# Six buffers instead of five for the residual rows of a graph-attention layer that runs ahead of a slice mixer

## The chip, the cores and the metric

The kernel runs on one core of a Trainium2 chip. The metric is the device time of one launch in microseconds, the median over several runs. TensorE does matrix products and transposes, VectorE and ScalarE work elementwise, GpSimd (POOL in the profile) does small powers and issues the gathering, casting and accumulating transfers, and SyncE (SP) issues the other transfers.

## What is computed

Two layers over `x` (32 batches of 512 rows of 256 numbers, float32), with an adjacency matrix of 512 x 512 integers for each batch:

```python
# layer 0
x = x + relu(layernorm(x) @ W_upd + mean_over_neighbours(layernorm(x) @ W_msg) + bias)
x = x + ffn(layernorm(x))            # tropical max-plus branch gated with a GELU branch
# layer 1
x = x + graph_attention(layernorm(x), adj)   # 4 heads of 64, softmax over neighbours,
                                             # relu + residual, layernorm per head
x = x + slice_mixer(layernorm(x))            # softmax of rows to 64 slices for each of 8 heads,
                                             # a scan over the 64 slice tokens, rows back from slices
```

Within one batch, layer 1 needs all 512 rows of layer 0's result. The batches are independent.

## The kernel before, in words

`layer0_sorted` computes layer 0 with the rows sorted, and writes them to DRAM tensors `x2s`; `ranks` holds where each row went. `layer1_plain` (L865) computes layer 1 and writes `out`. A general version of both layers stands behind a condition at the end and does not run on these inputs. The change is in `layer1_plain` alone.

Layer 1 handles the 32 batches by pairs (`GB = 2`). The mixer of pair g, `mixer(g)`, calls `slices(b)` for its two batches, then `tokens` and `scan` for both together, then `unslice(b)` for each. Beside it, `attentions()` runs ahead: for each batch `prepare(b)`, `attention(b)` and `norm(b)`, with the attention of batch b mixed step by step with the preparation of batch b + 1 by `woven`. The mixer's steps earn credit (`PACE`, L896), and each unit of credit advances `attentions()` by a step (L1581 to L1589). So the program's order is fixed when it is built; a tile scheduler then sets the semaphores, and the order of each engine's instructions does not change at run time.

What the steps do, with the lines that matter here:

- `prepare(b)`, L1136 on: takes a tile `x` of [128, 4, 256] float32 (512 KB, 4 KB in each partition) that holds the residual rows of the batch, and gathers the rows with four indirect transfers on POOL (L1142). `turn(b)` (L1091, SP) transposes the adjacency mask, and `shorten(b + 2)` (L1085, POOL) copies the adjacency of a later batch to a shorter type, as tile `short`. Then a normalisation: statistics `stc`, `mvc` on VectorE (L1114, L1115), the deviation `rsc` on POOL (L30, L31), `shiftc` on VectorE (L1119), the normalised rows `hv` on ScalarE (L1121). `add_rows` (L953, POOL) adds the vector BETA to the residual rows with an accumulating transfer. Transposes x3T (L1130, L1131) and the projection `hp` (L1171) follow; for each of four row tiles ScalarE makes `hv`, `mine`, `other` and `ht` (L1174 to L1179) and VectorE scales `hv` (L1175). `own` is sent to DRAM and read back for each of four heads as a broadcast (L1190, SP).
- `attention(b)`: weights `att` on VectorE (L1201), products `avp` and `adp` on TensorE (L1237, L1242), back-transposes `dp` and `bp` (L1220), `av` on VectorE (L1265), and another `add_rows` into `av`.
- `norm(b)`, L1274 on: the norm of each head, on VectorE (L1282 to L1286, L1290, L1291, L1293, L1295), with a square on ScalarE (L1288) and a power on POOL (L1292, tile `mu`). Last, L1296 adds the rows `av` to the residual tile `x`.
- `slices(b)`: normalisation as above with tiles `std`, `mvd`, `rsd`, `shiftd`; transposes x4T; `add_rows` with OUTB; for each of four row tiles t the logits `lgp` on TensorE (L1327), the exponential on ScalarE (L1328) and the softmax on VectorE (L1329, L1332, L1333, L1334, tile `sw`); then `yTp` (L1339), which contracts the rows of a batch against `sw`, for two halves c of the features, and the transposes `swp` (L1344).
- `tokens` and `scan`: projections and a scan over the slices, among them the transposes `oTp` (L1527) near the end.
- `unslice(b)`: products `outp` (L1559), added to the residual tile (L1561), and one store of 512 KB to `out` (L1562, SP). Then b is put in the set `stored` (L1563).

The residual tile of a batch lives from its gather to its store. `AHEAD_X` is the number of these tiles, and it also holds a preparation back in the program's order:

```python
while b >= AHEAD_X and b - AHEAD_X not in stored:
    yield True
xt = xs[b] = sb.tile([P, NT, D], F32, tag="x", name=f"x{b}", bufs=AHEAD_X)
```

A step that yields True gives the turn away: `woven` goes on with the attention alone, and when that has ended too, the credit is set to zero. With five tiles, batch 2g + 5 is prepared after the first store of pair g, and batch 2g + 6 after the second.

Of the kernel before, what the change touches and what calls it, by code (L numbers as in the profile page):

```python
# [864 lines left out]
def layer1_plain(tc, ident, eps, x2s, ranks, adj, w, out, over, ps):  # L865
# [6 lines left out]
    GB = 2  # L872
# [19 lines left out]
    AHEAD = 3  # L892
    ATT = 2 * (AHEAD + 2) + AP + 1
    HW = P // AH
    AHEAD_X = 2 * GB + 1
    PACE = 1.04 * GB * (TURNS + STEPS) / WANTED  # L896

    SMALL = 30.0 * 30.0 / D
# [2 lines left out]
    with ExitStack() as ctx:  # L901
# [234 lines left out]
        def prepare(b):  # L1136
# [4 lines that stand above are left out]
            for t in range(NT):  # L1141
# [1007 lines left out]
def tile_kernel(ctx, tc, ins, out):  # L2149
# [21 lines left out]
    with tc.tile_pool(name="few", bufs=1) as few:  # L2171
        over = few.tile([P, n0 + n1], F32, tag="over", name="over")
        NSEG = 4
        x2s = [dram.tile([len(x2) // NSEG * N, D], F32, tag=f"x2s_{i}", name=f"x2s_{i}") for i in range(NSEG)]
        ranks = few.tile([P, len(x2) * NT], I32, tag="ranks", name="ranks")
        rest = []

        def following(ps):
            rest.append(layer1_plain(tc, ident, eps2, x2s, ranks, ins["adj"], w1, out, over[:, n0:], ps))
            return iter(lambda: next(rest[0]), True)  # L2180

        layer0_sorted(tc, ident, eps2, ins["x"], ins["adj"], w0, x2s, ranks, over[:, :n0], following)
        for _ in rest[0]:
            pass


        ones = few.tile([P, 1], F32, tag="ones", name="ones")
        nc.gpsimd.memset(ones, 1.0)
        worst = few.tile([P, 1], F32, tag="worst", name="worst")
        nc.vector.tensor_reduce(worst, over, AX.X, ALU.add)  # L2190
        with tc.tile_pool(name="pf", bufs=1, space=PSUM) as ps:
            pf = ps.tile([P, N], F32, tag="flag", name="flag")
            nc.tensor.matmul(pf[:1, :1], worst, ones, start=True, stop=True)
            nc.vector.tensor_copy(again, pf[:1, :1])
# [36 lines left out]
```

## Time and profile before

| what | value |
| --- | --- |
| three runs | 4503.5, 4513.17, 4514.52 us; median 4513.17 |
| the profiled execution | 4515.02 us, its span 4513.3 us, mean granted clock 0.94 |
| TensorE busy | 3933.4 us, 87% of the span |
| VectorE, ScalarE, POOL busy | 3204.0, 2198.0, 1570.2 us |
| layer 1, 2372.0 to 4513.3 us | TensorE busy 1906.2 us in all |
| of it 2600 to 4272 us (steady) | TensorE 1520.4, VectorE 1080.1, ScalarE 725.3, POOL 356.3 of 1672 us; DMA share 0.33 |
| transfers over the span | 524.04 MB, mean 116 GB/s |

How to read it: the span runs from the first to the last instruction; the time of the execution has a little around it. "Busy" counts an engine's instructions without what they wait for. A group's line gives line, engine, operation, output<-input tiles, shapes and count, then busy us, mean ns of one, and the idle time just before them with the instruction that ended it. In a timeline, a line gives start, duration, engine, line and operation, and in brackets the idle time before it with its releaser. In the chain of waits, each piece gives start, duration and what ran; "issue" is time in which the engine waited for nothing that the profile shows. DMA pieces are transfers. The share of the DMA engines is the mean over the core's sixteen. The granted clock is TensorE's, 1.00 being full speed.

In the steady stretch one pair of batches takes about 129 us, and every such period has the same stages: the first slice, the second slice, the scan, and the two stores with the next gathers.

### The profile page before, as it was taken

What the parts mean: (1) busy time and instruction counts of PE and PEld (TensorE: products, weight loads), DVE (VectorE), ACT (ScalarE), POOL (GpSimd) and SP (SyncE); (2) the same over time, 40 slices, a digit from 0 to 9 for tenths busy, and PEclk for the clock granted to TensorE, in tenths of its full rate; (3) what the DMA queues carried; (4) which work ended last, traced back from release to release, by engine and by line L of the source; (5) the groups of instructions that cost most, each with busy time, mean ns of one, the idle gap of its engine ahead of it and who ended that gap; (6) DMA issues with size and microseconds to landing.
All of it is one profiled execution on the core that took longest, in us unless ns stands there. A gap on an engine that the chain in (4) does not pass through costs nothing.

```text
span 4513.3 us, 56135 instructions
## 1 busy us (share of the span) xinstructions
PE 3933.4 (87%) x19799; PEld 2468.0 (55%) x19799; DVE 3204.0 (71%) x6909; ACT 2198.0 (49%) x4305; POOL 1570.2 (35%) x2069
## 2 busy tenths in 40 slices
PE   5567898899988999889997999898998898989987
PEld 4454565656656656555553555555555455555555
DVE  6678888897788877867765766656666666666663
ACT  3345565556565665545663444344444443444433
POOL 2356544664446554444313122222211222222110
PEclk8778999999999999989998999999999999999998
DMA  5546543664446643564315233333322333333210
GB/s 129 160 142 224 184 140 110 206 202 154 135 129 206 194 141 109 169 216 160 129 59 117 52 76 79 80 80 68 83 68 62 73 80 80 80 70 76 62 38 20
DMA packets 301248, 524.04 MB, mean 116 GB/s; under 512 B 104823, under 2 KB 180227, under 8 KB 300956
## 3 DMA queue, kind: packets, MB, share of 16 engines
q0 software_dynamic: 117120, 383.06, 30.6%
q1 hardware_dynamic: 183836, 137.30, 10.4%
q8 instruction: 158, 2.59, 0.2%
q14 instruction: 134, 1.10, 0.1%
HBM read 463.11 MB, written 73.95 MB: 119 GB/s over the span
## 4 chain that ended last, share of the span: by engine, by line
PE 32%; DVE 31%; DMA 15%; issue 9%; POOL 8%; ACT 4%; SPq 1%; DVEq 0%; POOLq 0%; ACTq 0%
DVE acc L637 4%; PE clsp L623 4%; PE po L652 4%; DMA av<-added 3%; PE yTp L1339 3%; PE gatep L623 3%; PE outp L1559 3%; POOL mu L1292 2%; DMA rows<-table,xs 2%; DMA out<-x 2%; DMA rows<-table,tops 2%; DVE best L598 2%; PE oTp L1527 2%; DVE att L1201 2%; PE avp L1237 2%
## 5 line engine op out<-in xcount | busy, mean ns | idle before, releaser
L623 PE MATMUL clsp<-xnT,wc 128*128 128x512 f32 x1024 | 524.8, 631 | 46.7 <-ACT cls L625 34.4
L623 PE MATMUL gatep<-xnT,wg 128*128 128x512 f32 x1024 | 496.8, 605 | 9.3 <-ACT gate L625 9.3
L652 PE MATMUL po<-wd,acc 128*128 128x256 f32 x2048 | 457.3, 382 | 8.4 <-DVE acc L641 5.9
L652 PEld LDWEIGHTS po<-wd,acc 128*128 128x128 f32 x2048 | 389.2, 192 | 75.2 <-issue 9.6
L1201 DVE SCALAR_TENSOR_TENSOR att<-own,other,mask 128x512 f32<-128x512 f32 x512 | 358.3, 737 | 12.8 <-DMA own<-ownd 12.8
L598 DVE SCALAR_TENSOR_TENSOR best<-rows,xs,best 128x1024 f32<-128x1024 f32 x212 | 272.6, 1288 | 126.8 <-ACT best L592 79.5
L637 DVE SCALAR_TENSOR_TENSOR acc<-past,fld,acc 128x512 f32<-128x512 f32 x448 | 344.6, 772 | 23.8 <-ACT past L636 16.0
L1237 PE MATMUL avp<-att,hv 128*32 128x512 f32 x2048 | 333.0, 601 | 7.2 <-DVE att L1201 7.2
L1339 PE MATMUL yTp<-sw,x 128*128 128x512 f32 x512 | 262.1, 666 | 88.0 <-DVE sw L1334 88.0
L623 PEld LDWEIGHTS gatep<-xnT,wg 128*128 128x128 f32 x1024 | 196.8, 196 | 253.3 <-issue 203.5
L632 ACT ACTIVATE acc<-tz,fld 128x512 f32<-128x512 f32 x256 | 198.7, 776 | 279.1 <-PE tz L630 247.4
L636 ACT ACTIVATE past<-tz,fld 128x512 f32<-128x512 f32 x448 | 291.5, 693 | 79.3 <-DVE acc L637 77.7
L595 POOL DMA_INDIRECT rows<-table,xs x212 | 251.5, 1186 | 170.3 <-DVE best L598 117.3
L623 PEld LDWEIGHTS clsp<-xnT,wc 128*128 128x128 f32 x1024 | 183.9, 200 | 185.9 <-issue 114.1
L434 PE MATMUL pm<-h,adj 128*128 128x258 f32 (+1 forms) x1024 | 182.9, 326 | 103.9 <-DVE keep L427 42.6
L1327 PE MATMUL lgp<-wsl,x4T 128*128 128x512 f32 x512 | 241.3, 617 | 22.4 <-ACT x4T L1131 22.4
L625 ACT ACTIVATE gate<-gatep,fld 128x512 f32<-128x512 f32 x256 | 175.4, 685 | 146.4 <-PE gatep L623 124.0
L553 POOL DMA_INDIRECT xs<-rows_of,order x128 | 156.7, 1225 | 215.3 <-DVE acc L637 93.3
L1339 PEld LDWEIGHTS yTp<-sw,x 128*128 128x128 f32 x512 | 104.9, 214 | 227.5 <-DVE sw L1334 126.2
L1559 PE MATMUL outp<-v,swT 128*128 128x256 f32 x1024 | 226.2, 379 | 0.0
L434 PEld LDWEIGHTS pm<-h,adj 128*128 128x128 f32 x1024 | 152.8, 215 | 129.2 <-issue 73.4
L625 ACT ACTIVATE cls<-clsp,fld 128x512 f32<-128x512 f32 x256 | 176.0, 687 | 95.3 <-PE clsp L623 58.8
(593 smaller groups left out, 8550.7 us busy)
## 6 DMA issues: line engine op xcount, KB each, us to landing
adj<-in_adj POOLq DMA_DIRECT2D x128, 256.0 KB
x<-added POOLq DMA_DIRECT2D x64, 512.0 KB
own<-ownd SPq DMA_DIRECT2D x128, 256.0 KB
rows_of<-keep SPq DMA_DIRECT2D x32, 550.0 KB
x<-in_x SPq DMA_DIRECT2D x32, 512.0 KB
x2s<-xs SPq DMA_DIRECT2D x32, 512.0 KB
short<-in_adj POOLq DMA_DIRECT2D x32, 512.0 KB
av<-added POOLq DMA_DIRECT2D x32, 512.0 KB
```

Of the source, the lines that this page charges most:

```text
L434: nc.tensor.matmul(pm[:, : c1 - c0], a[:, i, t * P : (t + 1) * P], h[:, i, c0:c1], start=i + c0 == 0, stop=i + 1 == NT and c0 > 0)
L595: nc.gpsimd.indirect_dma_start(out=row, out_offset=None, in_=table, in_offset=bass.IndirectOffsetOnAxis(ap=idxs[:, k : k + 1].bitcast(U32) ...
L598: nc.vector.scalar_tensor_tensor(m, row, vals[:, k : k + 1], m, ALU.add, ALU.max)
L623: nc.tensor.matmul(pf, wf[:, c, f * P : (f + 1) * P], xnT[:, c, :], start=c == 0, stop=c == DC - 1)
L625: nc.scalar.activation(o, pf, fn, bias=fld[:, f, bf : bf + 1], scale=1.0 if fn == AF.Gelu else 0.5)
L636: nc.scalar.activation(r, z, AF.Relu, bias=fld[:, f, AT + b : AT + b + 1])
L637: nc.vector.scalar_tensor_tensor(y, r, fld[:, f, CH + b : CH + b + 1], y, ALU.mult, ALU.add)
L652: nc.tensor.matmul(po[:, i, :], acc[f][:, t * P : (t + 1) * P], wd[:, f, :], start=f == 0, stop=f == FC - 1)
L1201: nc.vector.scalar_tensor_tensor(e, own[h], other[:, j, h : h + 1], mask[:, j, :], ALU.max, ALU.mult)
L1237: nc.tensor.matmul(pv[p][k * HW : (k + 1) * HW, :], hv[:, j, h, e : e + HW], weighed[b, h, j], **ends)
L1339: nc.tensor.matmul(py, xn[:, t, c * P : (c + 1) * P], sw[:, t, :], start=t == 0, stop=t == NT - 1)
L1559: nc.tensor.matmul(po[:, :D], swT[:, k, t * P : (t + 1) * P], v[:, k, :], start=k == 0, stop=k == KC - 1)
```

## The change

One constant grows by one. The tile pool holds six residual tiles, 24 KB of each partition where it held 20, and `prepare(b)` waits for the store of batch b − 6 where it waited for that of b − 5. For batch 2g + 6 that is the first store of pair g. Batch 2g + 7 waits for the second store of pair g; it waited for the first store of pair g + 1 before. Batch 5 waits for no store. What `prepare` yields, and what the steps compute, stays the same; the places of the other steps on the engines follow from the order in which the generators are advanced.

```diff
@@ -892,7 +892,7 @@
     AHEAD = 3
     ATT = 2 * (AHEAD + 2) + AP + 1
     HW = P // AH
-    AHEAD_X = 2 * GB + 1
+    AHEAD_X = 2 * GB + 2
     PACE = 1.04 * GB * (TURNS + STEPS) / WANTED
 
     SMALL = 30.0 * 30.0 / D
```

## The prediction on record

> **What bounds the kernel now.** I read the page first (span, slices, groups), then the waits of TensorE in layer 1, then one pair end by the chain of waits and by the timelines of the engines. The page gives a span of 4513.3 us and this group:
>
> ```profile
> L1339 PE MATMUL yTp<-sw,x 128*128 128x512 f32 x512 | 262.1, 666 | 88.0 <-DVE sw L1334 88.0
> ```
>
> It is the largest idle time of TensorE that is put down to one line of layer 1. The edit touches only `layer1_plain`, which runs from the first gather (L1142, at 2372 us) to the end: some 2141 us. Between 2600 and 4272 us TensorE is busy for 1520 of 1672 us, so it is the bound there, and what counts is what it waits for. Its waits in that stretch (total us, times, longest) begin with:
>
> ```profile
> PE yTp L1339 <- DVE sw L1334: 82.8, 18, 7.5
> PE lgp L1327 <- ACT x4T L1131: 19.5, 13, 3.4
> PE minep L1183 <- ACT mine L1177: 16.8, 13, 1.3
> ```
>
> Nearly all of the 82.8 us lies in one place that comes back every 129 us or so: the end of a pair, where `unslice` has stored two batches and the next pair's first slice starts. The chain of waits through the pair end near 3000 us shows what is late (start, duration, what):
>
> ```profile
> 2990.35 6.86 DMA out<-x
> ...
> 3001.85 0.95 POOL x L1142
> 3002.80 0.61 POOL short L1085
> 3003.40 2.97 POOL mu L1292
> ...
> 3007.54 0.42 DVE stc L1114
> 3007.96 1.12 DVE x L1296
> 3009.09 1.20 DVE sw L1329 x2
> ...
> 3011.71 0.61 DVE sw L1334
> 3012.32 0.04 issue
> 3012.37 9.30 PE yTp L1339 x16
> ```
>
> The reader is to see one queue behind another. POOL waits for the second store of the pair (`out<-x`), because its next gather reuses that buffer. Behind the four gathers stand the adjacency copy `short` and only then the power `mu` of an attention's norm; VectorE waits for `mu`, and the softmax weights `sw` that TensorE needs are queued on VectorE behind it. The timelines give the two idle times, VectorE's and then TensorE's:
>
> ```profile
> 3006.40 1.22 DVE L1295 TENSOR_TENSOR av<-av,mu 128x1024 f32<-128x1024 f32 x1 [8.79 <-POOL mu L1292]
> ```
>
> ```profile
> 3012.37 9.30 PE L1339 MATMUL yTp<-sw,x 128*128 128x512 f32 x16 [6.42 <-DVE sw L1334]
> ```
>
> At thirteen pair ends this idle time is 3.1, 6.0, 6.3, 6.4, 5.9, 6.1, 7.2, 6.6, 6.5, 7.5, 6.5, 6.7 and 5.3 us; at a fourteenth, near 4290, it is 1.7.
>
> [...] `mu` has its input from 2996.2 us on and starts at 3003.40, directly behind the gathers and `short`. [...] granted clock 0.50 or 1.00, a fall 3.1 to 4.9 us after TensorE stops at twelve pair ends, full speed again 3.6 to 6.0 us after it restarts.
>
> **The change, part by part.** I compared the instruction orders of the two kernels. No instruction is added or dropped; some are moved.
>
> *At a pair end.* Before, the batches gathered are an odd one (after the first store) and the next even one (after the second). With six buffers the odd one was gathered a pair earlier, so the two are the even one (first store) and the next odd one (second store). The wait for the second store stays: POOL's gathers still stand ahead of `mu`. Three things leave the path from the second store to `yTp`:
> - `short` goes behind `mu`: −0.60 us (0.61 in the chain).
> - One `stc` statistic, L1114, no longer stands between L1295 and L1329: −0.34.
> - L1296 goes behind all four groups of `sw`: −1.12. It adds an attention's rows to a batch that the next pair needs, so it has time.
>
> Together −2.06 us. Against it: TensorE's order of `yTp` becomes all four row tiles of one half, then of the other. The third tile of `sw` is ready 3.75 us after the first (L1334's second pair of instructions starts at 15.46 against 11.63, from the timeline of VectorE, with 0.64 for one); the four instructions of the first two tiles take about 3.5 at half clock (16 instructions in 7.21 at full clock are 0.45 each, so about 0.9 at half): 0.25 us of waiting. Net −1.8 us for each of 12 pair ends. From `yTp` the chain runs on TensorE to 3033.8 almost without a break, so I count it in full. At the first pair end the idle time is split in two and the clock does not fall; I take −1.2. At the last, near 4290, no odd batch is left to gather; `stc` and its L1115s go from before L1291 (some 1.7 us of VectorE, half of it beside other waits): −1.2 (0 to −1.7).
>
> *What is paid for it.* The odd batch's normalisation (ScalarE, L1121 x4, 2.07 us) moves into the scan, where ScalarE is idle for 1.60 us before L1174 at 3088.30, and its BETA add (POOL, 0.5 MB) moves behind the other add of the scan. I cost both at nothing: the idle time hides the first but for some 0.1 to 0.5 us, and VectorE's idle time of 7.90 us before 3096.86 hides the second. If that cover is gone, see the fourth case. SP's queue keeps its order.
>
> *At the start.* Batch 5 is now gathered at once. Four gathers and a `short` enter POOL at about 2414.5 us, ahead of an add and the L30/L31 of batch 3: 4 x 1.25 (their spacing there) + 0.6 = 5.6 us, and 0.5 MB of rows and 1 MB of adjacency read beside `own<-ownd`, for which the first attention waits:
>
> ```profile
> 2414.53 1.04 POOL L953 DMA_DIRECT2D x<-added  x1
> 2415.36 0.43 POOL L30 TENSOR_TENSOR rsc<-mvc,eps 128x4 f32<-128x4 f32 x1
> ```
>
> VectorE also meets the `stc` of batch 5 ahead of the first `att` at 2423.41, and so waits for those rows. The trace of before does not show this; bounds: +1.5 us (1.5 MB more at the page's mean would take far longer, but most of it is not waited for) to +6 (the whole POOL block and 0.35 of L30/L31). I take +3.4, nearer the middle.
>
> *Sum.* −(1.2 + 12 x 1.8 + 1.2) + 3.4 = −20.6 us, against the profiled execution's 4515.02: 4494.4. That execution lies 1.85 us above the median of the three runs (4513.17), so the forecast for the median is 4492.6.
>
> **The rivals.**
> - *A: given back.* Only `short` is gained; `stc` and L1296 are only moved, and the odd slice of the pair, which waits for VectorE's queue, pays them back. For it: they are 1.46 us of the same engine, and after 3016 VectorE works on the odd batch's `std`. Against it: TensorE does not wait for the odd slice's `yTp` at 3041.97, and x4T has some 4 us there. −12 x 0.6 + 3.4 = −3.8: 4509.4.
> - *B: the clock helps.* The idle time drops from 6.4 to about 4.3 us[...]; and the transposes `oTp` (L1527) in the scan take 5.47 us at 7 of the first 14 pairs, with the clock falling, and 3.84 at the other 7. If the shifted phase frees all of them: 7 x 1.63 = 11.4 us, and a kept clock at `yTp` some 0.3 x 12 = 3.6 (little, since the third `sw` tile then sets the pace). −20.6 − 15 = −35.6: 4477.6. [...]
> - *C: slower, a collision in the scan.* The moved BETA add (`av<-added`, of the same size, lands in 5.25 us) shares the DMA engines with the four `own<-ownd` of 256 KB issued at 3091.51; the DMA share is already 0.61 to 0.64 there. `att` at 3096.94 has about 1.8 us to spare, so the attention turns late once `own` lands more than 1.8 us later, and the kernel loses once it is more than 1.8 + 1.8 = 3.6. With the full 5.25: 3.45 − 1.8 = +1.65 per pair, +19.8 in 12, −2.4 at the two other ends, +3.4: +20.8, so 4533.9. Against it: the add starts some 3 us ahead of `own`, and most of it is then through.
>
> **How the numbers follow.** Forecast 0.60, A 0.20, B 0.11, C 0.09. The forecast's own range, 4484 to 4502, comes from the start (1.5 to 6), 1.5 to 2.1 us per pair end, and a few `oTp` that gain or lose their clock. The whole range must take in A, and B's mean: 4478 to 4511, which leaves out C and half of B. Some 0.3% of the time, 13.5 us, is what a measurement of this kernel can tell from no change: faster is below 4499.6. That holds nine tenths of the forecast's chance (0.54) and B: 0.65. Same: the rest of the forecast, A and a small part of C: 0.27. Slower: 0.08.
>
> **What would show it.** Right: at a pair end POOL's `mu` directly behind the fourth gather, `short` after it, L1329 directly behind L1295, TensorE's idle time before the even `yTp` near 4.3 us and the period 1.8 us shorter; the first `att` some 3 us later. Wrong: an idle time of 4.3 with an unchanged period (A: look for the wait that grew); `oTp` at 3.84 throughout (B); `att` in the scan waiting for `own<-ownd` (C). A second store that lands later, because the gathers compete with it, would void the whole sum.

## The result, and the profile after

Median 4487.52 us (13 runs, 4479.3 to 4493.71) against 4510.43 us for the kernel before on the same occasions (13 runs): a ratio of 0.9948, 95% interval 0.9937 to 0.9958, so 23.5 us faster (19 to 28). The forecast was 20.6 us.

The two profiled executions differ by more, 4513.3 against 4483.2 us of span. Of these 30 us, 7.0 lie ahead of the first gather of layer 1 (2372.15 against 2365.17), in code that the change does not touch; over the eleven profiled executions of this document that point lies anywhere from 2355.6 to 2373.8. From the first gather to TensorE's last instruction it is 2132.65 against 2109.09 us: −23.6, the size of the measured gain.

The page's groups after: the wait of `yTp` for `sw` is smaller, and VectorE now waits for `own`, which took 12.8 us in all before.

```profile
L1201 DVE SCALAR_TENSOR_TENSOR att<-own,other,mask 128x512 f32<-128x512 f32 x512 | 360.3, 741 | 37.4 <-DMA own<-ownd 37.3
...
L1339 PE MATMUL yTp<-sw,x 128*128 128x512 f32 x512 | 258.1, 653 | 72.6 <-DVE sw L1334 72.4
```

TensorE's waits from 2599 to 4250 us (total, times, longest), where 82.8 stood for `yTp` and 19.5 for `lgp`:

```profile
PE yTp L1339 <- DVE sw L1334: 67.9, 27, 5.4
PE lgp L1327 <- ACT x4T L1131: 23.8, 13, 4.1
PE minep L1183 <- ACT mine L1177: 16.9, 13, 1.3
```

The chain of waits through the same pair end, now at 2982 to 3007 us:

```profile
2982.60 7.03 DMA out<-x
...
2994.32 0.95 POOL x L1142
2995.27 0.03 issue
2995.30 2.95 POOL mu L1292
2998.25 0.02 issue
2998.27 1.23 DVE av L1295
2999.50 1.20 DVE sw L1329 x2
```

The second store is still there, and so are the four gathers that wait for it. But `mu` follows the fourth gather directly (the copy `short` follows `mu`), and the softmax weights follow L1295 directly: `stc` and L1296 are gone from between. POOL's timeline shows that its wait for the store has grown, as it now has less to do beforehand, and TensorE's shows what is left of its idle time:

```profile
2990.41 0.98 POOL L1142 DMA_INDIRECT x<-x2s,ranks  x1 [8.50 <-DMA out<-x]
...
2995.30 2.94 POOL L1292 TENSOR_TENSOR mu<-mu,eps 128x16 f32<-128x16 f32 x1
2998.21 0.62 POOL L1085 DMA_DIRECT2D short<-in_adj  x1
```

```profile
3002.78 9.25 PE L1339 MATMUL yTp<-sw,x 128*128 128x512 f32 x16 [5.18 <-DVE sw L1334]
```

One more thing came out of the instruction orders. A kernel with six tiles in the pool and the gate of `prepare` left at five has, on every engine, the very instruction order of the changed kernel. So, unlike what the source suggests and the description above repeats, the gate moves nothing here. The tile count does: with it alone the gathers change places.

### The profile page after: what moved, and what is told of

The parts are those of the page before. It is cut to its first block, busy times and chain, and to the rows that moved or that the text cites. A ratio compares the mean times of both kernels' runs of the same rounds, so it can differ in the third digit from the quotient of the medians.

```text
span 4483.2 us, 56051 instructions
## 1 busy us (share of the span) xinstructions
PE 3906.9 (87%) x19799; PEld 2445.7 (55%) x19799; DVE 3200.8 (71%) x6909; ACT 2198.9 (49%) x4305; POOL 1561.5 (35%) x2069
## 4 chain that ended last, share of the span: by engine, by line
DVE 32%; PE 27%; DMA 16%; issue 10%; POOL 9%; ACT 6%; SPq 1%; DVEq 0%; POOLq 0%; another core or an unknown queue 0%; ACTq 0%
DVE acc L637 4%; PE clsp L623 3%; DMA av<-added 3%; PE gatep L623 3%; DVE att L1201 3%; DMA rows<-table,xs 2%; PE po L652 2%; PE yTp L1339 2%; POOL mu L1292 2%; DVE best L598 2%; PE outp L1559 2%; DMA rows<-table,tops 2%; PE avp L1237 2%; POOL x L1142 2%; PE hp L1171 2%
```

## The experiments

The theory: what counts is what stands, on POOL and VectorE, between the second store and the first `sw` ("order"). The first rival: the odd batch is gathered and normalised a pair earlier, and that time is the gain ("prefetch"). If order is right, five tiles must do as well. Where a kernel needed another order, its source was given edges of issue order (`tc.issue_after(x)` queues what it encloses behind x on the same engine, with no wait for its end), or a step was put behind other yields. No kernel leaves work out.

All times below marked "after outp" count from the first `outp` product of a pair, and are means over eleven pair ends (those of the third to thirteenth even slice) out of the timelines; the period is the mean of the eleven from the second even `yTp` to the thirteenth. Each ratio is to runs of the kernel before on the same chip (medians 4510.43 for the changed kernel, 4509.87 for e1 to e4, 4506.9 for e5 to e7, 4505.08 for e8 and e9); "us faster" is worked out from the ratio and 4510.

| kernel | second gathers start | `mu` ends | even `yTp` starts | idle before it | pair's period | median us | ratio to before (95%) |
| --- | --- | --- | --- | --- | --- | --- | --- |
| before | 24.97 | 33.40 | 39.40 | 6.52 | 128.59 | 4510.43 | |
| changed | 25.13 | 32.86 | 37.40 | 4.95 | 126.56 | 4487.52 | 0.9948 (0.9937 to 0.9958) |
| e1 copies away, 5 tiles | 22.41 | 31.27 | 37.28 | 3.79 | 126.57 | 4484.77 | 0.9941 (0.9922 to 0.9959) |
| e2 VectorE order, 5 tiles | 24.85 | 33.26 | 37.81 | 4.93 | 126.95 | 4487.61 | 0.9946 (0.9928 to 0.9963) |
| e3 both, 5 tiles | 23.68 | 32.55 | 37.09 | 1.65 | 125.59 | 4476.54 | 0.9928 (0.9908 to 0.9949) |
| e4 gathers behind `mu`, 5 tiles | 26.78 | 26.60 | 35.46 | 2.61 | 123.47 | 4438.45 | 0.9829 (0.9807 to 0.9851) |
| e5 first copy away, 5 tiles | 22.18 | 31.67 | 37.67 | 4.51 | 126.28 | 4482.34 | 0.9946 (0.9930 to 0.9962) |
| e6 = e4 + e2, 5 tiles | 26.78 | 26.60 | 32.70 | 0.0 | 119.53 | 4384.03 | 0.9721 (0.9705 to 0.9738) |
| e7 both gathers behind `mu`, 6 tiles | 32.96 | 25.47 | 31.73 | 0.0 | 121.82 | 4412.92 | 0.9794 (0.9776 to 0.9813) |
| e8 second gathers behind `mu`, 6 tiles | 26.28 | 26.09 | 32.15 | 0.0 | 119.39 | 4387.69 | 0.9740 (0.9717 to 0.9763) |
| e9 copies in the scan, 6 tiles | 24.59 | 32.44 | 37.74 | 0.16 | 125.42 | 4466.12 | 0.9912 (0.9892 to 0.9932) |

**e1: the copies away.** Both `short` of a pair end are issued before its stores; only POOL's order changes.

```diff
-            shorten(b + 2)
             yield
             yield
             yield
+            shorten(b + 2)
```

> Five tiles as before; both adjacency copies (tile short) of a pair are moved out of the pair end, into the scan ahead of it. Only POOL's order differs. Order theory (what stands in POOL's and VectorE's queues between the second store and the first sw is the whole gain): the copy leaves the path, 0.6 us at each of 13 pair ends, so 7 to 8 us faster than before, mu starting directly behind the fourth gather, about 4.8 us after the first one starts. Prefetch theory (the gain comes from the odd batch being gathered and normalised a pair earlier, which needs a sixth tile): no change, within 3 us of before.

Measured: 26.6 us faster (ratio 0.9941), more than three times the expectation. The prefetch theory fails, as no sixth tile is there, but the order theory had the size wrong: not 0.6 but 2.1 us per pair end. The second gathers start 2.56 us sooner, and POOL no longer waits for the store ahead of them at all:

```profile
2991.71 1.05 POOL L31 TENSOR_TENSOR rsc<-rsc,eps 128x4 f32<-128x4 f32 x1
2992.96 2.03 POOL L1142 DMA_INDIRECT x<-x2s,ranks  x1 [0.19 <-issue]
...
2998.87 2.94 POOL L1292 TENSOR_TENSOR mu<-mu,eps 128x16 f32<-128x16 f32 x1
```

The idle time of 0.19 before the gather says that the store had landed when POOL came to it, and it is 0.19 at all eleven pair ends. Before, that gather waited for the store:

```profile
2997.98 1.05 POOL L1142 DMA_INDIRECT x<-x2s,ranks  x1 [3.11 <-DMA out<-x]
```

What holds POOL now is the odd batch's `rsc`. That points to a copy as what had held up the store; e5 tests it. (From there to `mu` it is 5.9 us, not the 4.8 that the expectation named: the first gather takes 2.03 us instead of 1.05.)

**e2: VectorE's order.** L1296 and the even batch's statistics behind the four `sw` groups. With it TensorE's order of the even `yTp` becomes that of the changed kernel, one half of the features after the other.

```diff
+            with tc.issue_after(weights[b - 4].ins) if b % GB == 0 and b - 4 in weights else ExitStack():
-            normed(xt, xn, f"c{b}")
+                normed(xt, xn, f"c{b}")
...
+            with tc.issue_after(weights[b - 1].ins) if b - 1 in weights else ExitStack():
-            nc.vector.tensor_add(xt, xt, rows)
+                nc.vector.tensor_add(xt, xt, rows)
...
-                nc.vector.tensor_mul(s, s, st.unsqueeze(2).to_broadcast([P, H, G]))
+                weights[b] = nc.vector.tensor_mul(s, s, st.unsqueeze(2).to_broadcast([P, H, G]))
```

> Five tiles as before; on VectorE, L1296 and the statistics of the even batch are queued behind the four sw groups instead of ahead of them. POOL's copies stay where they are. Order theory: L1329 follows L1295 directly, 0.34 + 1.12 = 1.46 us less at each of 13 pair ends, minus up to 0.25 of waiting for the third sw tile: 16 to 19 us faster than before. Prefetch theory: no change, since the even batch's statistics come later and nothing comes earlier; within 3 us of before. Given-back theory (the odd slice pays for L1296): 0 to 5 us faster, with the odd yTp waiting.

Measured: 24 us faster (17 to 32). From the end of `mu` to `yTp` it takes 4.55 us instead of 6.00: the 1.46 expected, to the hundredth. Nothing of it is given back. The prefetch and the given-back theories both fail. The rest of the 24 us, some 5, is of the size of the changes at the edges of the layer and in the scan's clock (1.63 us for each slow `oTp`), and is not resolved by the interval.

**e3: both.** The edits of e1 and e2 together.

> Five tiles as before, with both moves: the copies out of the pair end and L1296 and the even batch's statistics behind sw. Order theory: the two add up to 2.06 us at each of 13 pair ends, so 24 to 27 us faster than before, equal to the changed kernel or 1 to 4 us better, as nothing is paid at the start of the layer. Prefetch theory: less than a quarter of the changed kernel's 23 us.

Measured: 0.9928, or 32 us faster (23 to 41). Five tiles do at least as much as the sixth tile did (0.9948; the intervals overlap). But e1 and e2 alone would add up to 51 us. The idle time before `yTp` fell by 4.9 us to 1.65, the period only by 3.0: the last output addition (L1561) came 18.5 us after outp where it had been 16.9. VectorE had waited 3.4 us for `own` in the scan ahead of it (timeline of VectorE, start, duration, and the wait in brackets):

```profile
2960.67 2.74 DVE L1202 SCALAR_TENSOR_TENSOR att<-own,other,mask 128x512 f32<-128x512 f32 x4 [3.36 <-DMA own<-ownd]
```

The copies were now ahead of `own`: from the write of `own`'s rows to the first `att` it takes 8.8 us, against 6.1 before.

**e4: the wait for the store behind mu.** The even batch's gathers are queued behind the power.

```diff
+            held = powers.get(b - 3 - b % GB)
+            with tc.issue_after(held.ins) if held else ExitStack():
-            for t in range(NT):
-                nc.gpsimd.indirect_dma_start(
+                for t in range(NT):
+                    nc.gpsimd.indirect_dma_start(
...
+            powers[b] = nc.gpsimd.tensor_tensor(mu[:, 1, :], mu[:, 1, :], eps[:, 1:2].to_broadcast([P, NG]), ALU.pow)
```

> Five tiles as before; the second batch of gathers at a pair end is queued on POOL behind the power mu instead of ahead of it, so that mu no longer stands behind the wait for the second store. VectorE's order stays as before, with one statistic of the gathered rows still ahead of sw. Order theory: mu ends near 2999.2 instead of 3006.4 on the scale of the profile of before, the statistic then waits for its rows until about 3002.5, and yTp starts 4 to 5 us earlier; TensorE's idle time falls to about 2 us[...] and yTp takes some 2 us less: about 6 us at each of 13 pair ends, 65 to 85 us faster than before. Theory that the store itself is the bound (the gather is late anyhow and the attention waits for it): under 25 us faster, with the wait moved to the even batch's preparation.

Measured: 77 us faster, as the order theory had it. `mu` ends at 26.6 after outp instead of 33.4, `yTp` starts 3.9 us sooner in its pair, and with 2.6 us of idle time instead of 6.5 the even `yTp` takes 8.4 to 8.8 us at nine of the eleven where it took 9.1 to 10.1. At most of the nine, 0.99 of it is a wait for the third `sw` tile, and the 7.4 to 7.8 us left there are near the 7.21 us that the 16 instructions take in the trace of before at a granted clock of 1.00. The mean granted clock of the profiled execution is 0.953, against 0.940 before. The period falls by 5.1 us. The gathers start 1.8 us later, and one instruction misses them: the statistic that still stands ahead of `sw` now waits for their rows, and from the end of `mu` to `yTp` it takes 8.86 us instead of 6.00.

```profile
2985.29 0.43 DVE L1114 BATCH_NORM_STATS2 stc<-x 128x6 f32<-128x256 f32 x1 [2.73 <-DMA x<-x2s,ranks]
```

**e5: the first copy alone.** Only the odd batch's `short` moves; the second stays ahead of `mu`.

```diff
-            shorten(b + 2)
+            if b % GB == 0:
+                shorten(b + 2)
             yield
             yield
             yield
+            if b % GB:
+                shorten(b + 2)
```

> Five tiles as before; only the first adjacency copy of a pair end (the odd batch's, issued while the two stores are under way) is moved into the scan; the second copy stays ahead of mu. Queue-only theory: the first copy is not on the path, since POOL waits for the second store behind it anyway: no change, within 4 us. Competition theory (formed on the first experiment, where the second batch of gathers started 2.56 us sooner after the first output product): the copy's traffic delays the second store, so the second gathers start about 22.4 us after the first output product instead of 25.0, and the kernel is 15 to 22 us faster, 0.6 us per pair end short of the first experiment.

Measured: 24 us faster (17 to 32), second gathers at 22.18. The landings say it directly. In the chain of waits the second store takes 6.0 to 8.0 us from issue to landing at the twelve pair ends of before that have it (6.86 at the one in the prediction). Where the trace of e5 holds its landing, at three pair ends, it takes 3.1 to 3.2. In e9 below, which moves both copies and where POOL waits for the store again, it takes 2.9 to 3.6 at thirteen pair ends, as here:

```profile
2974.42 3.15 DMA out<-x
```

The competition theory is right: a transfer that nobody on the path waits for delayed one that all wait for. Which part of the transfer does it (its reads, its writes, its packets) was not tried.

**e6: e4 and e2 together.**

> Five tiles as before; the second gathers queued behind mu, and on VectorE L1296 and the even batch's statistics behind sw: the two edits that worked alone. Order theory: the statistic that waited for its rows is gone from the path, yTp can start 4.55 us after mu ends, at about 31.2 us after the first output product where the fourth experiment had 35.5, but TensorE itself is busy until about 32.9: idle time near 0, about 2.5 us less per pair end than the fourth experiment, 4400 to 4412 us. Theory that the bound passes to the scan (the attention waiting for own): 4425 or more, with VectorE waiting there for own.

Measured: 4384.03 us, 0.9721 (0.9705 to 0.9738), some 126 us faster than before, and better than the expectation. TensorE goes from `hp` to `yTp` without a wait (its timeline; the line numbers are shifted by the edits):

```profile
2968.01 1.16 PE L1174 MATMUL hp<-wa,x3T 128*128 128x264 f32 x4
2969.00 1.88 PE L1344 MATMUL yTp<-sw,x 128*128 128x512 f32 x4
2971.35 5.42 PE L1344 MATMUL yTp<-sw,x 128*128 128x512 f32 x12 [0.46 <-DVE sw L1339]
```

`yTp` takes 7.8 us from its start to its end instead of 9.5, and the granted clock is 1.00 from 2942 to 2990 us. The 2.5 us expected over e4 became 3.9 per pair: 2.8 up to the start of `yTp`, and 1.2 after it, which was not counted; 1.0 of that is `yTp` itself (means of 8.74 and 7.76).

**e7: six tiles, all gathers of the pair end behind mu.** The edit of e4 on the changed kernel.

> Six tiles, with both batches of gathers of a pair end queued on POOL behind mu. In the instruction order the first sw group then stands ahead of L1295 on VectorE, so that TensorE need not wait for mu at all. Order theory: idle time before the even yTp near 0, as in the sixth experiment, 4400 to 4415 us, the sixth tile adding nothing or costing 0 to 10 us by its BETA add in the scan (VectorE waiting 2 us for own, as in the changed kernel). Prefetch theory (a sixth tile gives time of its own): at least 10 us faster than the sixth experiment.

Measured: 4412.92 us, at the upper end of the order theory's range, and 29 us slower than e6 where prefetch asked for 10 us faster. The pair end is as good (idle 0.0), but the rest of the pair is longer: from the even `yTp` to the next `outp` 90.09 against 86.83 us. Part of it is seen in TensorE's waits for `sw`, 27.2 us against 8.0 over some twelve pairs, now mostly at the odd slices; the rest was not followed up (the mean granted clock of the profiled executions is 0.953 here and 0.956 in e6).

**e8: six tiles, only the second gathers behind mu.** As e7 with `held = powers.get(b - 4) if b % GB else None`.

> Six tiles; only the second batch of gathers of a pair end, the one that waits for the second store, is queued on POOL behind mu. VectorE's order at the pair end is that of the changed kernel. This is the sixth experiment with a sixth tile. Order theory: idle time before the even yTp near 0 and yTp 32.7 us after the first output product, as there; a sixth tile adds no time of its own, so 4384 to 4400 us, a few of them from its start and from its BETA add in the scan. Prefetch theory: under 4374. Collision theory (with the pair end gone, own in the scan is on the path, as the third experiment's later stores hint): 4400 to 4415, with the last output addition more than 1 us later than the 16.8 us after the first output product.

Measured: 4387.69 us, 0.9740, against 0.9721 for e6: the intervals overlap. Once the order is right, the sixth tile is worth nothing that can be measured. The collision theory fails here (last output addition at 16.88).

**e9: six tiles, copies in the scan.** The edit of e1 on the changed kernel.

> Six tiles; both adjacency copies of a pair end are moved into the scan, ahead of the odd batch's BETA add, so that all three transfers stand in front of own. Only POOL's order differs from the changed kernel. Competition theory alone: the second gathers start 2.5 us sooner at 13 pair ends, 28 to 33 us faster than the changed kernel, about 4455 us. Rival C of the prediction, with its threshold: from the write of own's rows to the first att it took 6.1 us before, 7.5 in the changed kernel, 8.7 in the first experiment; three transfers make it 10 or more, beyond the 3.6 us that the prediction named, so the output additions come 1.5 to 3 us later and half or more of the gain is given back: 4470 to 4490 us.

Measured: 0.9912 against the changed kernel's 0.9948, some 16 us better, where the gain without a collision would be 28 to 33. From the write of `own`'s rows to the first `att` it takes 11.0 us, 4.9 more than before; VectorE waits for it:

```profile
2954.66 2.74 DVE L1201 SCALAR_TENSOR_TENSOR att<-own,other,mask 128x512 f32<-128x512 f32 x4 [3.55 <-DMA own<-ownd]
```

The last output addition comes at 20.2 after outp, 3.2 us later than in the changed kernel, a little past the range given, and about half of the gain is gone. The median of 4466 lies just under the range expected of the rival; on the scale of 4510 that the other gains are given on, it is 4470, the edge of that range.

## Why the prediction was right

**The path at the pair end.** `short`: forecast −0.60, measured −0.67 (from the second gathers' start to `mu`, 5.46 to 4.79 us). `stc` and L1296: forecast −1.46, measured −1.46 (from the end of `mu` to `yTp`, 6.00 to 4.54), and e2 shows the same alone. They are two separate terms, each with its own edit, and each was sized from one line of the chain.

**What was taken off for TensorE's order, 0.25.** The wait for the third `sw` tile is there (0.21 to 0.66 us at eight of twelve pairs, 0.23 in the mean). But the even `yTp` takes only 0.12 us longer from start to end (9.46 to 9.58), because less of it runs at half clock (4.1 us of it instead of 4.7). The net per pair was forecast at 1.8 and is 23.60/12 = 1.97: the −2.13 of the two terms, and a store that lands 0.1 to 0.2 later.

**Counting the rest in full.** From the even `yTp` to the next `outp` it takes 89.16 us against 89.19: nothing was given back and nothing gained. That is in part luck, since changes of a few us in twelve pairs cancel in it: `oTp` −4.9, waits for `x4T` and `rn` +5.9.

**The idle time was forecast at 4.3 and is 4.95.** TensorE finishes its own work 0.43 us sooner as well (39.40 − 6.52 against 37.40 − 4.95), so the idle time shrinks less than the path. The path is what counts.

**Start and ends.** The forecast of the start and first pair end was +3.4 − 1.2 = +2.2; measured from the first gather to the second even `yTp`: 256.1 to 258.9 us, +2.8. That these are close is luck, as both terms were off. At the start VectorE does wait for the rows of batch 5, as said, but the first `att` comes 2.0 us later, not 3.4, and the delay up to the first `outp` is 2.6 us (0.6 of it ahead of the first `yTp`). The first pair end gains nothing (+0.2): the prediction took it that the clock does not fall there, and in the changed kernel it is at half for 3.4 us, so that `yTp` takes 9.25 us instead of 8.39. Near 4290 us: −1.2 forecast, −1.1 measured. Not foreseen are −1.7 us in the last pair and the tail.

**Two readings** in the prediction are slightly off and move no term: by the two starts that it gives, the third `sw` tile is 3.83 us behind the first, not 3.75; and the clock's own record has the falls at 3.4 to 4.9 us after TensorE stops and full speed 4.0 to 6.1 us after it restarts.

**Rival A (given back)** fell: e2 keeps its gain. **Rival B (clock)**: the clock still falls at `yTp`, and `oTp` was slow at 4 of the first 14 pairs instead of 7. In the other kernels it was slow at anything from one (e3, e6) to ten (e1) of the first thirteen, and each time costs 1.63 us. (`oTp` is a product with `hoT`, not a set of transposes, as it is called above.) At each of the seven `oTp` of 5.4 to 5.5 us in before the granted clock is 0.50 for 3.41 us, from between 0.07 us ahead of `oTp` and 0.83 us after its start, and over the seven others it is 1.00. The scan keeps TensorE waiting several times in a short stretch ahead of `oTp`, here at one of those seven:

```profile
3085.31 1.87 PE L1509 MATMUL yp<-xk,mix 64*64 64x64 f32 x32 [0.65 <-DVE mix L1502]
3087.11 1.16 PE L1171 MATMUL hp<-wa,x3T 128*128 128x264 f32 x4
3089.56 0.28 PE L1183 MATMUL minep<-ident,mine 128*16 128x128 f32 x1 [1.30 <-ACT mine L1177]
3089.68 0.62 PE L1519 MATMUL yTp<-ident,y 128*128 128x128 f32 x4
3091.02 5.47 PE L1527 MATMUL oTp<-yT,hoT 128*128 128x128 f32 x32 [0.73 <-ACT yT L1521]
```

That stretch does not tell the seven from the others: from the second pair on, TensorE is busy for 73 to 74% of the 10 us ahead of `oTp` and idle for at most 1.3 us at a time, at all seven and at the six others. Neither those idle times nor that share says which `oTp` will be slow; what decides it, and whether it is the shifted phase that the prediction supposes, was not shown.

**Rival C (collision in the scan)** is real, and costs next to nothing here. In the changed kernel the transfers of `own` are issued 2.6 us later (1.56 to 4.15 us after the write of its rows); if the landings, which these two traces do not hold, move as much, that lies between the prediction's two marks of 1.8 and 3.6. The attention does turn late: the first `att` comes 1.3 us later (6.13 to 7.47), and VectorE waits 0.2 to 3.2 us for `own` at every one of the eleven pairs, as here. But the last output addition moves by only 0.16:

```profile
2962.50 0.75 DVE L1201 SCALAR_TENSOR_TENSOR att<-own,other,mask 128x512 f32<-128x512 f32 x1 [2.02 <-DMA own<-ownd]
```

Counted from the first `outp`, the first `att` comes 1.6 us later than before in the changed kernel, 2.1 in e1, 3.4 in e3 and 5.4 in e9, and the last output addition 0.2, 0.4, 1.7 and 3.4 us later. So about 1.5 to 2 us of a late attention are free, and most of what goes beyond them is lost. The prediction had no such room: it took the loss to begin as soon as `att` is late.

**What the prediction did not see.** It took the landing of the second store as given. The store is late because an adjacency copy runs beside it (e1, e5: 6.0 to 8.0 us to its landing with the copy, 3.1 to 3.2 without), and that alone is worth as much as the whole change. And the sixth tile is only one way to the new order: e3 gets at least as much from five, and e6 far more.

## What to carry to other kernels

When a buffer count changes the time, look at which instructions change places before crediting the buffer: here it moved 2 us of work off one chain, and edges of issue order on five buffers gave five times as much. Read the queue of the engine that holds a wait: put the instruction that others need ahead of the one that waits, and keep transfers that nobody needs yet from running beside the one that all wait for. A transfer moved off the path lands in another stage, so check what is loaded there (here `own`) and how much slack its reader has.

## What the runs showed that was not expected

An adjacency copy (1 MB read, 0.5 MB written) beside a 512 KB store more than doubled the time from the store's issue to its landing (6.0 to 8.0 us, against 2.9 to 3.6 without it), and the store's waiter started 2.6 us later (24.97 against 22.41 us after outp). The power `mu` of 128x16 took 2.93 to 2.99 us at the thirteen pair ends of before, directly behind a DMA issue on POOL, and 3.33 us at those of e4 and e6, after an idle time; elsewhere it took 2.9 to 3.8. Where an accumulating transfer was issued 1.2 us ahead of a small write, the transfers that follow that write were issued 2.6 us later (4.15 us after the write's issue instead of 1.56). At the seven slow `oTp` of before TensorE's granted clock was 0.50 for 3.41 us, with no idle time of TensorE above 1.3 us in the 10 us ahead; at six other pairs it stayed at 1.00 after the same waits. At the twelve pair ends of before where TensorE was idle for 5.3 to 7.5 us the clock fell 3.4 to 4.9 us after it had stopped, and stayed at 0.50 for 6.8 us or, once, 10.2.
